# A higher place in the instruction order for carries, the last tile and finished node tiles in a max-pooling layer

## The chip, the cores and the metric

The kernel runs on one core of a Trainium2 chip. A core has several engines that run at the same time, each through its own fixed list of instructions: TensorE (PE in the profile, matrix products; PEld is its weight load), VectorE (DVE, element-wise work and scans), ScalarE (ACT, casts and copies), GpSimd (POOL, here mostly gathers of rows by index) and SyncE (SP, here a queue that starts transfers). Transfers run on 16 DMA engines. An instruction starts when it is its turn on its engine and the semaphores that it waits for have been set. The metric is the device time of one launch in microseconds (us); lower is better.

## The reference

The input is a graph of 6250 nodes with 256 features and 100000 edges, sorted by destination. A normalised copy of the features goes through four graph layers with 512 features between them, then a last product, and the input is added:

```python
def _sage_pool(h, src, dst, n, deg, W_pool, b_pool, W_self, W_neigh, b):
    hp = jax.nn.relu(h @ W_pool + b_pool)
    hmax = jax.ops.segment_max(hp[src], dst, num_segments=n)
    hmax = jnp.where(deg[:, None] > 0, hmax, 0.0)
    return h @ W_self + hmax @ W_neigh + b
...
deg = jax.ops.segment_sum(jnp.ones(edge_dst.shape[0], features.dtype), edge_dst, num_segments=n)
h = _sage_mean(features, edge_src, edge_dst, n, deg, W1_self, W1_neigh, b1)
h = _sage_pool(h, edge_src, edge_dst, n, deg, W2_pool, b2_pool, W2_self, W2_neigh, b2)
h = _sage_gcn(h, edge_src, edge_dst, n, deg, W3_neigh, b3)
h = _sage_mean(h, edge_src, edge_dst, n, deg, W4_self, W4_neigh, b4)
return h @ W_fc + b_fc
```

`_sage_mean` and `_sage_gcn` sum rows over the edges and multiply by weights. Layer 2, the max-pooling layer, takes for each node the maximum over the rows of its in-edges. The change lies in layer 2.

## The kernel before

**Tiles.** The nodes are 49 tiles of 128 rows. Layer 2 reads the row of each edge's source from a table in HBM with gathers of 128 rows (128x512 in float32); there are 782 of them, in six blocks of 52, 100, 220, 180, 130 and 100 gathers. The blocks are taken from the last to the first, so block 5 comes first and block 0 last.

**The loop over gathers.** In a block each of the 128 partitions walks along its own run of edges. A gather (line 1639, on POOL) brings one edge for each partition into `X`, and DVE keeps a running maximum over edges of the same destination (line 1620, function `step`): `run` is the maximum so far, `X` becomes what is stored. A buffer `X` holds two gathers; there are six such buffers. The results go to HBM on SP (line 1624).

**The carry.** A destination's edges can continue from one partition into the next. At a block's end, `carry(b, ...)` turns the last result of the block with PE (`ptcf`, line 1374), scans along the partitions on DVE (`segf`, `cTf`, lines 1387 and 1391), gathers the rows that are to be mended (`fixf`, line 1404, on POOL), turns the scan back on PE (`pcf`, line 1412; 1398 in block 0), takes the maximum (line 1415) and stores the rows (line 1416). In block 0 the rows stay in SBUF.

**Finished node tiles.** When the carry of a block is done, all node tiles whose first edges lie in it can be finished, by `done2(d)`: gathers of the tile's maxima (`tot`, line 1500), a turn (`pt_hTf`, line 1524), products with the weights (`pm_prf`, lines 1531, 1534, 1537), and a split of the result into three bfloat16 parts `hi`, `mid`, `lo` (casts on ACT at 1545, 1554, 1561, with a matmul that subtracts the part between them, 1551 and 1558). The parts are stored to `tab_r`, from which layer 3 reads. `last_done2(d)` does the same for tile 0, which needs block 0's carry: `pc_last` and `pt_last` bring in block 0 (lines 1476 and 1458), `pm_last` is the product (lines 1451, 1484, 1492).

**Early products.** Layer 3 needs, for each destination tile, the sum over source tiles of a matrix of edge counts times the rows that layer 2 has just finished. For 18 destination tiles and source tiles 10 to 41 this is done while layer 2 still gathers: always when four source tiles are finished, a batch of products is put on a list (`pd`, line 571, and 569 for the tile itself), 12 matmuls for each destination and batch. The counts `ae` are loaded on SP (line 1590), the sums are added to `acc3` on DVE (line 1296; the first batch is copied by ACT, line 1299). The finished rows of a tile lie in one of 11 places, `d % 11`, so tiles 2, 1 and 0 write where tiles 13, 12 and 11 of the last batch lay, which the last batch's products must have read.

**What sets the order.** The Python code is a set of generators, of which the loop over gathers takes a piece at a time; this gives each instruction a number, its place in the program. A scheduler then makes each engine's list by simulating readiness: among the instructions that are ready it takes the one with the lowest number. `tc.high_priority(offset=n)` lowers the numbers in its scope by `n`. Before the change no piece of carry, last tile or finished tile is raised by it in this stage, so they and the early products are taken in the order in which the loop emits them:

```python
for g in list(now):
    if next(g, 0) == 0:
        now.remove(g)
```

`now` holds the node tiles under way. Behind the loop, the rest of the generators is run out, and layer 3 begins, whose first loads and gathers (`zt`, line 1745; `ring`, line 488) wait for the last store to `tab_r`.

Of the kernel before, what the change touches and what calls it, by code (L numbers as in the profile page):

```python
# [77 lines left out]
def fast_path(  # L78
# [1012 lines left out]
    with ExitStack() as on:  # L1091
# [35 lines left out]
        def done1(d, acc):  # L1127
# [37 lines left out]
            with behind(ended):  # L1165
                for k in range(KI):
# [11 lines left out]
                        lambda acc, d=d: todo.append(done1(d, acc)), extra=3)  # L1178
# [127 lines left out]
    with tc.tile_pool(name="fl2c", bufs=1) as ck, ExitStack() as late:  # L1306
# [61 lines left out]
        top = late.enter_context(ExitStack())  # L1368
        wpool = top.enter_context(tc.tile_pool(name="fw2", bufs=1))

        def carry(b, last):
            pt = bank(pst, "pt", "ptcf")
            for k in range(KH):
                turn = nc.tensor.transpose(pt[:, k * P : (k + 1) * P],
                                           last[:, k * P : (k + 1) * P], ident)
            if b == 0:
                last_turn.append(turn)
                for f in between:
                    f(KI)
            yield  # L1380
            yield
            yield
            cT = wk.tile([P, KH, P], F32, name="cTf", bufs=1)
            for k in range(KH):
                seg = wk.tile([P, P + 1], F32, name="segf", bufs=2)
                nc.vector.memset(seg[:, 0:1], 0.0)
                nc.vector.tensor_tensor_scan(
                    seg[:, 1:], keepT[:, b, :], pt[:, k * P : (k + 1) * P], 0.0,
                    op0=ALU.mult, op1=ALU.max,
                )  # L1390
                nc.vector.tensor_mul(cT[:, k, :], seg[:, :P], contT[:, b, :])
                yield
            fix = wk.tile([P, FH], F32, name="fixf", bufs=1)
            if b == 0:
                pc = bank(psm, "pm", "pcf")
                for k in range(KH):
                    tc.keep_in_program_order(
                        nc.tensor.transpose(pc[:, k * P : (k + 1) * P], cT[:, k, :], ident))
                for f in between:
                    f(2 * KI)  # L1400
                nc.scalar.copy(fix, pc)
                carried.append(fix)
                return
            nc.gpsimd.indirect_dma_start(
                out=fix, out_offset=None, in_=rows2[0 : run_at[b] + n_of[b] - P, :],
                in_offset=bass.IndirectOffsetOnAxis(ap=fixI[:, b : b + 1], axis=0),
            )
            for _ in range(4):
                yield
            pc = bank(psm, "pm", "pcf")  # L1410
            for k in range(KH):
                nc.tensor.transpose(pc[:, k * P : (k + 1) * P], cT[:, k, :], ident)
            for _ in range(3):
                yield
            nc.vector.tensor_tensor(fix, fix, pc, op=ALU.max)
            nc.sync.dma_start(runs[b][n_of[b] - P :, :], fix)
            for _ in range(4):
                yield
# [212 lines left out]
        for b in reversed(range(NB)):  # L1631
            tb = BLOCKS[b]
            t0 = offs[b] // P
            run = psr.tile([P, FH], F32, name="run")
            for s0 in range(0, tb, G2):
                X = (xmore if at // G2 % 2 else xpool).tile([P, G2, FH], F32, name="X2")
                for k in range(G2):
                    t = t0 + s0 + k
                    nc.gpsimd.indirect_dma_start(  # L1639
                        out=X[:, k, :], out_offset=None, in_=tab_p,  # L1640
                        in_offset=bass.IndirectOffsetOnAxis(ap=srcI[:, t : t + 1], axis=0),
                    )
                    row, st = X[:, k, :], same[:, t : t + 1]
                    if s0 + G2 >= tb:
                        step(row, X[:, 0, :] if k else run, st, row)
                        if k:
                            stored(b, s0 // 2, X)
                    elif k == 0 and s0:
                        step(run, run, st, row)
                    elif k:  # L1650
                        held = run if s0 else X[:, 0, :]
                        if s0 == 0:
                            step(run, held, st, row)
                        step(X[:, 0, :], row, st, held)
                        if s0:
                            step(run, run, st, row)
                        stored(b, s0 // 2, X[:, :1, :])
                    at += 1
                    if at > 8:
                        next(steps, None)  # L1660
                        if todo and next(todo[0], 0) == 0:
                            todo.pop(0)
                    if at >= 130 and at % 12 == 0:
                        next(finding, None)
                    if at == MADE_AT:
                        for _ in steps:
                            pass
                        top.close()
                        early_pool.append(
                            top.enter_context(tc.tile_pool(name="early3", bufs=1)))  # L1670
                    if at <= EARLY_AT:
                        hub.advance(math.ceil(len(first) * max(0, at - 16) / (EARLY_AT - 16)))
                    if copies and not hub.left():
                        copies.pop(0)()
                    early.advance(early.done + math.ceil(
                        early.left() / max(1, min(32, T - 24 - at))))
                    if b == 0 and s0 == 0 and k == 0:
                        for _ in finding:
                            pass
                    if b == 0 and not tiles and not ends and last_tiles and at >= T - 14:  # L1680
                        now += [last_done2(d) for d in last_tiles]
                        last_tiles.clear()
                    if s0 + k > 2 and ends and next(ends[0], 0) == 0:
                        ends.pop(0)
                        tiles += [d for d in reversed(range(NT)) if b_of[d][0] == last_b]
                    if (tiles and not (b and ends) and at >= begun_at + (11 if b else 7)
                            and begun2 < NT * (at - FIRST_AT) / (T - 36 - FIRST_AT)):
                        begun_at = at
                        now.append(done2(tiles.pop(0)))
                        begun2 += 1  # L1690
                    for g in list(now):
                        if next(g, 0) == 0:
                            now.remove(g)
            end = carry(b, X[:, 1, :])
            next(end)
            ends.append(end)
            last_b = b
# [787 lines left out]
```

## Time and profile before

| | |
|---|---|
| time, median of 3 runs | 3219.61 us (3212.12 to 3224.33) |
| the profiled execution | 3232.3 us, span 3230.2 us |
| mean clock of TensorE that the throttle granted | 0.907 |
| busy: PE, DVE, POOL, ACT | 2547.1, 2082.5, 1915.0, 910.9 us |
| first and last gather of layer 2 | 852.9 and 2225.8 us from the span's start |
| last step of the running maximum | 2239.5 us |
| first gather of layer 3 | 2263.9 us |

Rows of the profile name the engine, the line, the operation and the tiles, output first (`pd<-kept_rows,ae`), then the number of instructions (`x30`). In a row of the timeline the first number is the start and the second the length, both in us; in brackets stands how long the engine was idle before and what ended that. In a list of waits the three numbers behind a row are total, times and longest. Ends of matmuls are modelled, so start-to-start distances are the safer measure of their pace. "remote" or "another core or an unknown queue" is a wait whose release the trace doesn't show; on one core it is no other core.

### The profile page before, as it was taken

The numbers are of one execution on the slowest core, as the hardware profiler recorded it, in microseconds if no ns is written. First come the engines' busy times: TensorE is split into PE (matmuls) and PEld (weight loads), VectorE is DVE, ScalarE is ACT, GpSimd is POOL, SyncE is SP. The second block draws the span as 40 slices with busy tenths as digits, with TensorE's granted clock in tenths as the row PEclk, the third lists the DMA queues.
The fourth block names the chain that finished last, engine by engine and source line by source line (L and its number), as shares of the span: only waits on it lengthen the run. The fifth ranks groups of instructions, "written<-read, shape, count | busy, mean of one in ns | idle before, by whom it ended". The sixth has DMA issues, their size and how long they took to land.

```text
span 3230.2 us, 39608 instructions
## 1 busy us (share of the span) xinstructions
PE 2547.1 (79%) x11759; PEld 1330.1 (41%) x11894; DVE 2082.5 (64%) x5526; ACT 910.9 (28%) x2192; POOL 1915.0 (59%) x2238
## 2 busy tenths in 40 slices
PE   4687888898566456587887788798899999888887
PEld 2245555566333222233333333344344444444443
DVE  8677656655567768756776778766356665355555
ACT  5455666653266757511010001011000011000000
POOL 5566666666454655655565556663666665666664
PEclk8799899999898677788998889899999999999998
DMA  8455566666687888878898889886999998767775
GB/s 265 142 169 157 170 176 176 185 186 177 203 284 260 265 266 283 298 261 265 279 297 260 276 269 300 282 273 228 331 325 342 336 348 284 235 200 202 204 205 167
DMA packets 352573, 793.55 MB, mean 246 GB/s; under 512 B 58414, under 2 KB 154134, under 8 KB 352316
## 3 DMA queue, kind: packets, MB, share of 16 engines
q0 software_dynamic: 143840, 502.78, 50.7%
q1 hardware_dynamic: 141208, 205.28, 17.7%
q10 hardware_dynamic: 67300, 82.87, 7.8%
q8 instruction: 96, 1.57, 0.2%
q14 instruction: 129, 1.06, 0.1%
HBM read 592.60 MB, written 198.91 MB: 245 GB/s over the span
## 4 chain that ended last, share of the span: by engine, by line
PE 56%; issue 12%; DVE 9%; another core or an unknown queue 7%; ACT 6%; DMA 5%; POOL 2%; ACTq 0%; SPq 0%; DVEq 0%; POOLq 0%
PE pd L571 16%; PE pg L510 10%; PE pd L563 5%; PE pm_prf L1537 3%; PE pd L564 3%; DVE run L1620 3%; PE pm_hp L1167 2%; PE pb L346 2%; PE pg L505 2%; PE pm_hp L1161 2%; PE pm_w L272 2%; DMA X<-rows,srcIf 2%; PE pm_prf L1531 1%; PE pm_prf L1534 1%
## 5 line engine op out<-in xcount | busy, mean ns | idle before, releaser
L1639 POOL DMA_INDIRECT X<-rows,srcIf x782 | 742.0, 949 | 525.1 <-issue 231.3
L488 POOL DMA_INDIRECT ring<-tab_h,srcT x474 | 454.8, 959 | 274.8 <-issue 97.6
L1620 DVE SCALAR_TENSOR_TENSOR run<-run,samef,X 128x512 f32<-128x512 f32 x758 | 572.2, 755 | 68.2 <-DMA X<-rows,srcIf 43.0
L510 PE MATMUL pg<-ring,hot 128*128 128x256 bf16 (+2 forms) x2348 | 507.4, 323 | 36.0 <-issue 20.8
L571 PE MATMUL pd<-kept_rows,ae 128*128 128x512 bf16 x1523 | 405.8, 403 | 123.5 <-DVE acc L1296 67.2
L541 DVE SCALAR_TENSOR_TENSOR acc<-pg,M,acc 128x256 f32<-128x256 f32 (+2 forms) x681 | 347.3, 535 | 149.9 <-PE pg L510 52.3
L488 POOL DMA_INDIRECT ring<-tab_r,srcE x314 | 309.8, 987 | 172.7 <-issue 70.2
L488 POOL DMA_INDIRECT ring<-tab_s,srcE x314 | 299.9, 955 | 183.0 <-issue 69.7
L571 PEld LDWEIGHTS <-ae 128*128 128x128 fp8e4 x1728 | 176.3, 102 | 395.0 <-issue 247.3
L510 PEld LDWEIGHTS <-hot 128*128 128x128 bf16 x2364 | 235.6, 100 | 244.1 <-issue 109.6
L563 PE MATMUL pd<-zt,ac 128*128 128x512 bf16 x837 | 296.4, 385 | 26.1 <-issue 23.8
L484 DVE TENSOR_SCALAR hot<-iota_bf,keyE 128x128 bf16<-128x128 bf16 x628 | 152.4, 271 | 252.3 <-PE pg L510 76.7
L1620 DVE SCALAR_TENSOR_TENSOR X<-X,samef,run 128x512 f32<-128x512 f32 x379 | 282.3, 745 | 33.3 <-DMA X<-rows,srcIf 16.8
L564 PE MATMUL pd<-zt,ac 128*128 128x256 bf16 x882 | 243.2, 276 | 24.9 <-issue 22.7
L1537 PE MATMUL pm_prf<-unf,hTf 128*128 128x512 f32 x384 | 203.0, 656 | 11.5 <-ACT hTf L1527 6.1
L571 PE MATMUL pd<-Z,A 128*128 128x256 bf16 (+1 forms) x1176 | 195.4, 283 | 16.9 <-issue 14.9
L338 ACT ACTIVATE hs<-ht,onef 128x128 bf16<-128x128 bf16 x396 | 153.7, 393 | 177.8 <-PE pb L346 99.4
L346 PE MATMUL pb<-hm,hs 128*128 128x392 bf16 x461 | 153.6, 350 | 50.0 <-DVE hm L340 21.0
L340 DVE TENSOR_SCALAR hm<-iota_w,mk 128x392 bf16<-128x392 f16 x461 | 151.2, 335 | 47.1 <-PE pb L346 20.9
L1296 DVE TENSOR_TENSOR acc<-acc,pd 128x512 f32<-128x512 f32 x126 | 86.0, 682 | 147.9 <-remote 99.4
L484 DVE TENSOR_SCALAR hot<-iota_bf,keyT 128x128 bf16<-128x128 bf16 x474 | 123.2, 271 | 82.9 <-PE pb L346 32.3
L571 PE MATMUL pd<-kept_rows,ac 128*128 128x512 bf16 x526 | 149.4, 386 | 7.6 <-issue 6.9
(379 smaller groups left out, 3766.1 us busy)
## 6 DMA issues: line engine op xcount, KB each, us to landing
rows<-X SPq DMA_DIRECT2D x385, 256.0 KB
tab_r<-kept_rows ACTq DMA_DIRECT2D x44, 384.0 KB
rows<-hpf SPq DMA_DIRECT2D x49, 256.0 KB
th<-tab_t ACTq DMA_DIRECT2D x49, 256.0 KB
X<-rows,srcIf POOLq DMA_INDIRECT x782
ac<-tab_a ACTq DMA_DIRECT2D x108, 112.0 KB
tab_t<-th SPq DMA_DIRECT2D x37, 256.0 KB
tab_h<-Z SPq DMA_DIRECT2D x16, 579.0 KB
```

The lines of the kernel that those rows point to most:

```text
L338: nc.scalar.activation(hots[0], t, AF.Relu, bias=one, scale=-1.0)
L346: nc.tensor.matmul(hold[0], hots[0], hots[1], start=(k == 0), stop=(k == k_of[w] - 1))
L484: nc.vector.tensor_scalar(hot[j], iota_b, keyT[:, j - jb : j - jb + 1], None, op0=ALU.is_equal)
L488: nc.gpsimd.indirect_dma_start(out=ring[:, j % deep, :], out_offset=None, in_=table, in_offset=bass.IndirectOffsetOnAxis(ap=srcT[:, j - jb ...
L510: mm = nc.tensor.matmul(pg[:, : F + c], hot[j], X[:, part * F : (part + 1) * F + c], start=(k == 0 and part == 2), stop=(k == n - 1 and pa ...
L541: nc.vector.scalar_tensor_tensor(acc[d], half, m, acc[d], op0=ALU.mult, op1=ALU.add)
L563: nc.tensor.matmul(hold[0], a, z[:, : 2 * F], start=(s == ss[0]), stop=False)
L564: nc.tensor.matmul(hold[0][:, :F], a, z[:, 2 * F :], start=False, stop=(s == ss[-1]))
L571: nc.tensor.matmul(hold[0][:, : F + c], a, z[:, part * F : (part + 1) * F + c], start=(s == ss[0] and part == 2 and s != own), stop=(s == ...
L1537: nc.tensor.matmul(pm, hT[:, c, :], un[:, c, :], start=False, stop=(c == KH - 1))
L1620: nc.vector.scalar_tensor_tensor(put, held, st, row, op0=ALU.mult, op1=ALU.max)
L1639: nc.gpsimd.indirect_dma_start(out=X[:, k, :], out_offset=None, in_=tab_p, in_offset=bass.IndirectOffsetOnAxis(ap=srcI[:, t : t + 1], axis=0),
```

## The change

A wrapper `soon` runs each piece of a generator with its numbers lowered, by 2000 where nothing is said, by 600 for finished node tiles. It is put around the carries, around tile 0's generator and around `done2` in the loop. Not wrapped are the early products, and the generators that start only behind the loop.

```diff
+        def soon(pieces, by=2000):
+            while True:
+                with tc.high_priority(offset=by):
+                    if next(pieces, 0) == 0:
+                        return
+                yield
+
         def carry(b, last):
...
                     if b == 0 and not tiles and not ends and last_tiles and at >= T - 14:
-                        now += [last_done2(d) for d in last_tiles]
+                        now += [soon(last_done2(d)) for d in last_tiles]
                         last_tiles.clear()
...
                         begun_at = at
-                        now.append(done2(tiles.pop(0)))
+                        now.append(soon(done2(tiles.pop(0)), 600))
                         begun2 += 1
...
-            end = carry(b, X[:, 1, :])
+            end = soon(carry(b, X[:, 1, :]))
             next(end)
```

Seven lines are added ahead of the rest, so a line above 1371 has a number higher by 7 after the change. Each engine runs the same instructions as before, in another order, and only inside layer 2. Three places show it.

PE at the end of layer 2, before the change. `ptcf` is the last carry's turn (block 0), `pcf` its way back, `pc_last`, `pt_last` and `pm_last` belong to tile 0, `pm_prf` and `pt_hTf` to the node tiles before it:

```order
L1537 MATMUL pm_prf_19869<-unf_10820,hTf_19862 128x512 x4
L1458 MATMUL pt_hTf_19939<-identf_96,tot_19909 128x128 x4
L1374 MATMUL ptcf_19969<-identf_96,X2_19963 128x128 x4
L1451 MATMUL pm_last_19913<-usA_10818,th2_19911 128x512 x2
L1398 MATMUL pcf_19994<-identf_96,cTf_19976 128x128 x3
L1551 LDWEIGHTS minus_b_103
L1551 MATMUL pm_prf_19869<-kept_rows_10802,minus_b_103 128x512
L1398 MATMUL pcf_19994<-identf_96,cTf_19976 128x128
L1451 MATMUL pm_last_19913<-usB_10819,th2_19911 128x512 x2
L1476 MATMUL pc_last_20005<-takes0_17112,fixf_19993 128x128 x4
```

After the change the same place begins so,

```order
L1381 MATMUL ptcf_19969<-identf_96,X2_19963 128x128 x4
L1458 MATMUL pm_last_19913<-usA_10818,th2_19911 128x512 x2
L571 LDWEIGHTS ae_19221
L571 MATMUL pd_19332<-kept_rows_10802,ae_19221 128x512
L1405 MATMUL pcf_19994<-identf_96,cTf_19976 128x128 x4
L1458 MATMUL pm_last_19913<-usB_10819,th2_19911 128x512 x2
```

and, 242 rows of early products further on, ends so:

```order
L571 LDWEIGHTS ae_19512
L571 MATMUL pd_19689<-kept_rows_10802,ae_19512 128x512
L1558 LDWEIGHTS minus_b_103
L1558 MATMUL pm_prf_19869<-kept_rows_10802,minus_b_103 128x512
L1483 MATMUL pc_last_20005<-takes0_17112,fixf_19993 128x128 x4
```

Between the turn and `pc_last` there are now 124 matmuls of early products, 112 of line 571 and 12 of line 569; before there was none.

DVE at the same place. The scans and products of the carry (`segf`, `cTf`) were followed at once by tile 0's maxima (`hTf`):

```order
L1387 TENSOR_SCALAR segf_19989<-keepTf_10825,ptcf_19969 128x128
L1391 TENSOR_TENSOR cTf_19976<-segf_19985,contTf_10826 128x128
L1391 TENSOR_TENSOR cTf_19976<-segf_19989,contTf_10826 128x128
L1479 TENSOR_TENSOR hTf_19914<-hTf_19914,pc_last_20005 128x512
L1482 TENSOR_TENSOR hTf_19914<-hTf_19914,pt_last_20011 128x512
```

After the change ten adds of early products stand between them, of which five rows are shown (the last two and the row behind them follow each other directly):

```order
L1398 TENSOR_TENSOR cTf_19976<-segf_19989,contTf_10826 128x128
L1296 TENSOR_TENSOR acc3_8_10792<-acc3_8_10792,pd_19332 128x512
L1296 TENSOR_TENSOR acc3_9_10793<-acc3_9_10793,pd_19364 128x512
...
L1296 TENSOR_TENSOR acc3_16_10800<-acc3_16_10800,pd_19632 128x512
L1296 TENSOR_TENSOR acc3_17_10801<-acc3_17_10801,pd_19689 128x512
L1486 TENSOR_TENSOR hTf_19914<-hTf_19914,pc_last_20005 128x512
```

Before, the last of all these adds stood 14 steps of the running maximum ahead of the last one; over the stage they stand some 65 steps later than before.

POOL behind the carry of block 4 (`fixf` is the carry's gather, `tot` those of finished tiles). Before, 30 gathers of edges lie between the carry's gather and the first `tot`; the row of `fixf` and the rows around the first `tot` are:

```order
L1404 DMA fixf<-rows_71,fixIf 128x512
L1639 DMA X_14472<-rows_71,srcIf 128x512 x2
L1639 DMA X_14452<-rows_71,srcIf 128x512 x2
...
L1639 DMA X_14647<-rows_71,srcIf 128x512 x2
L1500 DMA tot<-rows_71,rows_of_130 128x512
L1500 DMA tot<-rows_71,rows_of_131 128x512
```

After the change there are six:

```order
L1411 DMA fixf<-rows_71,fixIf 128x512
L1646 DMA X_14452<-rows_71,srcIf 128x512 x2
L1646 DMA X_14472<-rows_71,srcIf 128x512 x2
L1646 DMA X_14489<-rows_71,srcIf 128x512 x2
L1507 DMA tot<-rows_71,rows_of_130 128x512
L1507 DMA tot<-rows_71,rows_of_131 128x512
L1507 DMA tot<-rows_71,rows_of_130 128x512
L1507 DMA tot<-rows_71,rows_of_131 128x512
L1646 DMA X_14504<-rows_71,srcIf 128x512 x2
```

The gathers of finished tiles have moved closer to the carry's gather and stand in a row of four, and two pairs of edge gathers that were exchanged stand in program order.

## The prediction

> **What bounds the kernel now.** The change touches only layer 2's max-pool stage, so I read that stage, 1345 to 2245 us of the span, and the hand-over to layer 3 behind it. First the table by windows (busy time of each engine, granted clock, DMA share), the last three stretches of the stage:
>
> ```profile
> core 0: us, PE busy (x) PEld busy (x) DVE busy (x) ACT busy (x) POOL busy (x), PEclk, DMA share, GB/s
> ...
> 1345.00:1660.00 315.00, 245.81 (x857) 109.59 (x875) 215.82 (x306) 36.18 (x66) 180.20 (x191) 0.89 0.83 273
> 1660.00:2060.00 400.00, 329.06 (x1212) 147.86 (x1235) 298.92 (x439) 34.72 (x60) 235.20 (x249) 0.91 0.86 280
> 2060.00:2245.00 185.00, 152.64 (x489) 69.67 (x494) 125.90 (x198) 23.00 (x41) 106.28 (x113) 0.90 0.83 272
> ```
>
> No engine is full: PE is 78 to 83% busy, DVE 68 to 75%, POOL 57 to 59%, the DMA engines 83 to 86%. The same view by block of gathers, for the gathers of line 1639 alone (blocks 5, 4, 3, 2, 1, 0):
>
> ```profile
> 852.90:1031.90 179.00, 94.87 (x100) 0.85 0.81 267
> 1031.90:1269.50 237.60, 124.28 (x130) 0.68 0.82 269
> 1269.50:1588.40 318.90, 170.39 (x180) 0.83 0.84 277
> 1588.40:1967.60 379.20, 208.41 (x221) 0.92 0.86 279
> 1967.60:2146.00 178.40, 94.48 (x101) 0.89 0.86 279
> 2146.00:2225.80 79.80, 48.57 (x52) 0.91 0.86 286
> ```
>
> Time over gathers is 1.79, 1.83, 1.77, 1.72, 1.77 and 1.53 us for one gather. Blocks 5 and 4 run before the early products begin (about 1345), blocks 3 to 1 beside them, at no slower pace. So the early products do not set the pace of the gathers by themselves. The chain of waits between 1280 and 2264 says that it passes from engine to engine:
>
> ```profile
> by line: PE pd L571 21.3%; another core or an unknown queue 17.4%; issue 13.9%; DVE run L1620 8.4%; PE pm_prf L1537 8.1%; DMA X<-rows,srcIf 5.1%; PE pm_prf L1531 3.6%; PE pm_prf L1534 3.4%; DVE X L1620 3.3%; DMA rows<-X 2.2%; DMA zt<-tab_r
> ```
>
> And the waits in the same window, by engine (total us, times, longest):
>
> ```profile
> DVE acc L1296 <- remote: 99.4, 19, 13.4
> ...
> POOL X L1639 <- DVE run L1620: 80.0, 41, 8.6
> ...
> POOL X L1639 <- DMA rows<-X: 31.4, 29, 7.5
> ...
> PE pd L571 <- DVE acc L1296: 72.7, 17, 10.7
> ...
> PE pm_prf L1551 <- ACT kept_rows L1545: 17.9, 2, 13.7
> ...
> SPq L1590 <- remote: 147.8, 20, 13.8
> ```
>
> DVE stands before the add of an early product (L1296) and the max steps queue behind it; the gathers wait for a buffer that a max step frees; PE waits for DVE to empty a bank; SP waits to load a block of edge counts (L1590) with stores queued behind. It is a loop of waits with slack on every engine. The end of the stage is different, a plain chain (last max step on DVE, then PE, then the first gather of layer 3 on POOL):
>
> ```profile
> 2239.53 0.75 DVE L1620 SCALAR_TENSOR_TENSOR X<-X,samef 128x512 f32<-128x512 f32 x1
> ...
> 2245.79 0.60 PE L1374 MATMUL ptcf<-identf,X 128*128 128x128 f32 x4
> ...
> 2247.95 1.17 PE L1398 MATMUL pcf<-identf,cTf 128*128 128x128 f32 x4
> ...
> 2250.68 1.05 PE L1476 MATMUL pc_last<-takes,fixf 128*128 128x128 f32 x8
> 2251.57 0.60 PE L1458 MATMUL pt_last<-identf,tot 128*128 128x128 f32 x4
> ...
> 2253.37 3.70 PE L1484 MATMUL pm_last<-unf,hTf 128*128 128x512 f32 x8 [0.99 <-DVE hTf L1482]
> 2257.74 0.38 PE L1492 MATMUL pm_last<-kept_rows,minus_b 128*128 128x512 bf16 x1 [0.67 <-ACT kept_rows L1488]
> ...
> 2263.88 0.95 POOL L488 DMA_INDIRECT ring<-tab_r,srcE  x1 [18.86 <-DMA ac<-tab_a]
> ```
>
> From the end of the last max step (2240.3) to layer 3's first gather (2263.9) 23.6 us pass, in which no early product runs. The first 5.5 us are PE's backlog of finished node tiles before the last carry's turn (L1374).
>
> **The change, part by part.** It adds and removes no instruction. Carries and last tile go 2000 places up, finished tiles 600; what loses is the early products, on PE, DVE and SP.
>
> *The tail on PE.* In the new order 124 matmuls of early products (112 of L571, 12 of L569) stand between the last carry's turn and pc_last of tile 0; before there are none. Turn, pc_last and pm_last cannot start before the last max step, and the three last tiles write to rows that the last batch of early products still reads, so this work cannot slip behind. Its price is the spacing of runs of such matmuls, start to next start:
>
> ```profile
> 2030.54 6.64 PE L571 MATMUL pd<-kept_rows,ae 128*128 128x512 bf16 x30
> 2037.02 0.38 PE L1558 MATMUL pm_prf<-kept_rows,minus_b 128*128 128x512 bf16 x1
> ...
> 1704.87 10.64 PE L571 MATMUL pd<-kept_rows,ae 128*128 128x512 bf16 x41
> 1715.36 0.38 PE L1558 MATMUL pm_prf<-kept_rows,minus_b 128*128 128x512 bf16 x1
> ...
> 2261.33 5.64 PE L571 MATMUL pd<-kept_rows,ac 128*128 128x512 bf16 x18
> ```
>
> 6.48 / 30 = 0.216, 10.49 / 41 = 0.256, 5.64 / 18 = 0.313 us. I take 0.216, since the operands in the tail have long been loaded: 124 x 0.216 = 26.8 us. Bounds: 124 x 0.313 = 38.8 us above, and 20 us below, if a quarter of them runs while PE would wait for the scans and casts anyway. Behind the last product come the casts of tiles 2 and 1 into the freed rows; two round trips between PE and ACT at the 0.67 us of the row at 2257.74 add 1.3 us. What goes is the backlog, 5.5 us, because nothing but products is left there. The adds on DVE that now stand behind the last max step, ten of them, keep pace: one is 0.68 us,
>
> ```profile
> 2060.58 0.68 DVE L1296 TENSOR_TENSOR acc<-acc,pd 128x512 f32<-128x512 f32 x1
> ```
>
> and the twelve products that feed it are 12 x 0.216 = 2.6 us; the last add lies beside the casts. Sum of the tail: 26.8 + 1.3 - 5.5 = +22.6 us, bounds 20 + 1.3 - 5.5 = +16 and 38.8 + 1.3 - 5.5 = +35. The work ahead of layer 3's zt loads and gathers is otherwise the same, so all of layer 3 starts that much later after the last max step.
>
> A rule of the Trainium skill speaks for this term: "TensorE: Matmul & The Clock Gate", Part 3, says that matmuls start and end in program order, with no reordering. By it pc_last cannot pass one of the 124; were they free to wait, the tail would gain the 5.5 us. No row here shows a matmul passing another.
>
> *The carries.* Until its turn a block's last result occupies a sixth of the X buffers. Last max step and turn of blocks 3, 2 and 1:
>
> ```profile
> 1601.07 0.75 DVE L1620 SCALAR_TENSOR_TENSOR X<-X,samef 128x512 f32<-128x512 f32 x1
> ...
> 1661.39 0.60 PE L1374 MATMUL ptcf<-identf,X 128*128 128x128 f32 x4
> ...
> 1976.62 0.75 DVE L1620 SCALAR_TENSOR_TENSOR X<-X,samef 128x512 f32<-128x512 f32 x1
> ...
> 2060.95 0.60 PE L1374 MATMUL ptcf<-identf,X 128*128 128x128 f32 x4
> ...
> 2153.10 0.75 DVE L1620 SCALAR_TENSOR_TENSOR X<-X,samef 128x512 f32<-128x512 f32 x1
> ...
> 2199.51 0.60 PE L1374 MATMUL ptcf<-identf,X 128*128 128x128 f32 x4
> ```
>
> That is 60, 84 and 46 us, 190 in all, and the new order shortens it. But block 1's hold lies wholly in block 0, whose pace, 1.53 us, is the best of all; block 2's hold fills 84 of the 178 us of block 1, at 1.77 us, no slower than block 4 with no long hold (1.83). So I take 0. Bounds: a sixth of 190 = 32 us gained; nothing lost. Earlier carries let node tiles begin earlier, which moves work on PE but does not end anything, as the products behind them end last now: 0.
>
> *Finished tiles ahead of products.* On POOL the first gather of tot follows the carry's gather after 6, 6, 14, 6 and 20 other gathers, before it is 12, 30, 58, 56 and 42. POOL issues in order, so a tot gather whose carry is not yet stored stops the X gathers behind it. Five carries; at worst each waits for ten gathers' worth, 10 x 1.77 = 18 us, 88 us in all; at best 0, where turn, scan and max come as much earlier as their order says. They are all pieces of the same higher place, so I take 0 to 10 and put 5 into the sum. On PE, tiles now run with fewer products between a cast and the matmul on it: by the order 22 of 48 tiles have under 1.5 us of other matmuls between L1537 and L1551, before it is 9, and between L1551 and L1558 16 against 6. That is 23 more tight round trips, at 0.67 us 15 us of PE time, at 1.2 us (the 17.9 us above over the 15 tight ones of before) 28 us. PE is idle 17 to 22% of the stage anyway, so of these I count 0, with 28 as the bound. On DVE the adds of products come some 65 max steps later, and SP loads the counts some 20 stores later, which moves the waits of 99.4 and 147.8 us above: gain and loss are both open. I take 0; the bounds are half of 99.4 gained, 50, and PE's 72.7 us wait for DVE half as long again, 36 lost.
>
> *What goes out from ahead of the last turn.* 26.8 + 5.5 = 32 us of PE work. Where PE is in the chain for some 36% (pd and the three pm_prf) of the stage this could bring the last max step forward by 0.36 x 32 = 12 us, and by 32 at the most. I take 5, no more, since the gathers' pace was the same without products.
>
> **Sum.** +22.6 (tail) + 5 (POOL) - 5 (less PE work before) = +23 us. The profiled execution takes 3232.3 us with a span of 3230.2, the median of the runs is 3219.6: 3255 us by the profile's own time, 3243 by the median.
>
> **The rivals.**
> 1. *It evens out, about 3216.* If PE sets the pace after all, moving products to the tail moves time and adds none: the stage before gains the 26.8 us that the tail receives, and the backlog saves some more, -4. For it: PE and its release make up the larger part of the chain. DVE's waits on "remote" have no recorded releaser, and "Perfetto Trace Analysis", section "Tensor Engine Instruction", says that the end of a matmul is estimated by the profiler, while the release comes only when PSUM acknowledges its bytes. So PE may be fuller than the 82% shown. Against it: blocks without products are no faster.
> 2. *Faster, about 3193.* DVE's adds of products no longer stop the max steps. If half of the 99.4 us goes, the stage gains 50 and the tail gives back 23: -27. It decides the sign from 23 of the 99.4 us on, the measurable gain from 39. For it: the adds stand 65 steps later. Against it: their products stand later on PE too.
> 3. *Slower still, about 3271.* The tight round trips cost PE 28 us that come on top of the tail, if PE's idle time does not lie where they fall; or POOL stops before the tots.
> 4. *No change*, that instructions do not move, is excluded by the order.
>
> **How the numbers follow.** Forecast (+16 to +40 us, 3236 to 3260): 0.44. Rival 1: 0.24. Rival 2: 0.18. Rival 3: 0.14. Half a per cent, 16 us, is about what a measurement of this kernel can tell from no change. Slower by more: 0.44 + 0.14 = 0.58; same 0.24; faster 0.18. The range leaves out half of rival 2 and the upper third of rival 3: 3195 to 3282.
>
> **What would show it.** In the changed profile: over 20 us of L571 between the last ptcf and pc_last, and 42 to 58 us from the last max step to the first ring gather; the last max step within 15 us of 2240. Holds of blocks 3 to 1 under 30 us with the same 1.7 to 1.8 us for one gather would show that they cost nothing. If the gathers of blocks 3 to 1 come under 1.65 us, a loop of waits was opened and I am wrong on the fast side; if POOL waits over 10 us before tots, or PE's waits at L1551 (now L1558) sum to over 40, on the slow side.

## The result: slower by one and a half per cent

The changed kernel takes 3261.13 us (median of 4 runs, 3255.99 to 3277.54), the kernel before 3216.07 us (4 runs, 3212.12 to 3224.33). The ratio is 1.0148, 95% interval 1.0121 to 1.0175: 45 us slower. The forecast was slower by 23 us, 3243, with a range of 3195 to 3282. The profiled execution of the changed kernel takes 3277.5 us with a span of 3275.6, 45.4 us over that of the kernel before, so the two profiles show the same difference as the medians.

The end of layer 2 in the changed kernel's timeline (last max step on DVE, then PE, then the first gather of layer 3 on POOL; lines above 1371 are higher by 7):

```profile
2262.59 0.74 DVE L1627 SCALAR_TENSOR_TENSOR X<-X,samef 128x512 f32<-128x512 f32 x1
...
2263.48 0.63 PE L1381 MATMUL ptcf<-identf,X 128*128 128x128 f32 x4 [0.89 <-DVE X L1627]
...
2266.00 0.71 PE L1405 MATMUL pcf<-identf,cTf 128*128 128x128 f32 x4
...
2295.03 1.05 PE L1483 MATMUL pc_last<-takes,fixf 128*128 128x128 f32 x8
...
2298.37 3.70 PE L1491 MATMUL pm_last<-unf,hTf 128*128 128x512 f32 x8 [0.56 <-DVE hTf L1489]
...
2308.51 0.95 POOL L488 DMA_INDIRECT ring<-tab_r,srcE  x1 [40.49 <-issue]
```

From the end of the last max step (2263.3) to the first gather of layer 3 it is 45.2 us, before it was 23.6: +21.6. The last max step itself comes 23.1 us later than before (2262.6 against 2239.5). Together they are 44.7 of the 45.4 us; layers 3 and 4 add the rest. So about half of the loss is where the forecast put all of it, and half is in the gather phase, for which the forecast had summed to nothing.

The gather phase by stretches of the same view as before, and by block of gathers (line 1646):

```profile
1345.00:1660.00 315.00, 218.57 (x693) 96.93 (x706) 195.16 (x292) 54.28 (x104) 175.08 (x184) 0.85 0.79 262
1660.00:2060.00 400.00, 331.42 (x1209) 148.29 (x1230) 295.56 (x434) 34.88 (x62) 235.91 (x249) 0.92 0.85 275
```

```profile
851.30:1021.10 169.80, 95.06 (x100) 0.85 0.85 279
1021.10:1256.10 235.00, 123.60 (x131) 0.69 0.84 278
1256.10:1584.80 328.70, 170.86 (x181) 0.77 0.80 267
1584.80:1980.80 396.00, 208.65 (x220) 0.90 0.83 268
1980.80:2164.70 183.90, 95.58 (x101) 0.91 0.83 272
2164.70:2245.50 80.80, 48.51 (x51) 0.91 0.87 293
```

Blocks 5 and 4 are not slower; in this pair of traces they are 9 and 3 us shorter. Blocks 3, 2 and 1 take 328.7, 396.0 and 183.9 us where they took 318.9, 379.2 and 178.4: +32 us in the three blocks that run beside early products. In the second pair of traces, taken later (see the experiments), the same three blocks take 30 us more. Between 1345 and 1660 PE does 218.6 us of work where it did 245.8, 27 us less.

The holds of the X buffer are gone in blocks 3, 2 and 1, under 1 us each from the end of the last max step to the turn. In block 2 the two rows now start 1.3 us apart (84 before):

```profile
1985.48 0.75 DVE L1627 SCALAR_TENSOR_TENSOR X<-X,samef 128x512 f32<-128x512 f32 x1
...
1986.81 0.60 PE L1381 MATMUL ptcf<-identf,X 128*128 128x128 f32 x4
```

### The profile page after: what moved, and what is told of

The parts are those of the page before. It is cut to its first block, busy times and chain, and to the rows that moved or that the text cites. A ratio compares the mean times of both kernels' runs of the same rounds, so it can differ in the third digit from the quotient of the medians.

```text
span 3275.6 us, 39589 instructions
## 1 busy us (share of the span) xinstructions
PE 2547.2 (78%) x11759; PEld 1334.9 (41%) x11894; DVE 2088.2 (64%) x5526; ACT 910.8 (28%) x2192; POOL 1918.4 (59%) x2238
## 3 DMA queue, kind: packets, MB, share of 16 engines
q0 software_dynamic: 143840, 502.78, 49.8%
## 4 chain that ended last, share of the span: by engine, by line
PE 53%; issue 13%; DVE 10%; another core or an unknown queue 9%; ACT 5%; DMA 5%; POOL 2%; ACTq 1%; DVEq 0%; POOLq 0%; SPq 0%
PE pd L571 14%; PE pg L510 10%; PE pd L563 5%; DVE run L1627 4%; PE pd L564 3%; PE pm_w L272 3%; PE pm_hp L1167 2%; PE pb L346 2%; PE pm_hp L1161 2%; PE pg L505 2%; PE pm_prf L1544 2%; DVE X L1627 2%; POOL X L1646 2%; PE pm_prf L1538 1%
## 5 line engine op out<-in xcount | busy, mean ns | idle before, releaser
L1544 PE MATMUL pm_prf<-unf,hTf 128*128 128x512 f32 x384 | 188.5, 613 | 1.5 <-ACT hTf L1534 1.2
L390 PE MATMUL pb<-hm,hs 128*128 128x196 bf16 x320 | 64.0, 303 | 120.1 <-ACT A L395 47.1
```

The source lines that it names most:

```text
L1544: nc.tensor.matmul(pm, hT[:, c, :], un[:, c, :], start=False, stop=(c == KH - 1))
```

## The experiments

They ran in three series of four, which the record lists under three different chips. The kernel before takes 3183.73, 3182.87 and 3185.47 us in them, and each ratio is against the runs of the kernel before in the same series. Each run has one trace, so a stretch of a trace is weaker evidence than a ratio. The edits are against the changed kernel unless it is said otherwise.

**Is it the products that stand behind the last turn?** The wrapper is taken off the last tile:

```diff
-                        now += [soon(last_done2(d)) for d in last_tiles]
+                        now += [last_done2(d) for d in last_tiles]
```

> The wrapper is taken off the last tile alone; carries and finished tiles keep it. The orders of POOL and SP are those of the changed kernel in every row, those of PE, DVE and ACT up to the last 10 us of the stage; no early product stands behind the last carry's turn any more, they stand ahead of it. Theory (124 products wait in the tail while PE had time for them before): the stretch from the last max step to layer 3's first gather goes back from 45 us to about 24 and the time from 3261 to about 3239. Rival (PE is behind with its work when the last max step comes, so the same products then delay the turn instead): the stretch stays at 42 to 50 us and the time at 3255 to 3265.

Measured: 3224.40 us, ratio 1.0142 (1.0091 to 1.0194). The end of layer 2 in its timeline:

```profile
2217.26 0.74 DVE L1627 SCALAR_TENSOR_TENSOR X<-X,samef 128x512 f32<-128x512 f32 x1
...
2242.87 2.11 PE L571 MATMUL pd<-kept_rows,ae 128*128 128x512 bf16 x9
...
2246.09 0.66 PE L1381 MATMUL ptcf<-identf,X 128*128 128x128 f32 x4 [0.28 <-ACT hTf L1475]
...
2251.12 1.05 PE L1483 MATMUL pc_last<-takes,fixf 128*128 128x128 f32 x8
...
2264.16 0.94 POOL L488 DMA_INDIRECT ring<-tab_r,srcE  x1 [41.44 <-DMA ac<-tab_a]
```

The products now stand ahead of the turn, and the turn waits for them: it comes 28.1 us after the end of the last max step, and from there to the first gather it is 46.2 us, where the changed kernel has 45.2. The rival was right. The place of the products behind the turn costs nothing by itself; in both orders PE still has them to do when the last max step is done.

**Which of the three wrappers?** Carries alone first:

```diff
-                        now.append(soon(done2(tiles.pop(0)), 600))
+                        now.append(done2(tiles.pop(0)))
...
-                        now += [soon(last_done2(d)) for d in last_tiles]
+                        now += [last_done2(d) for d in last_tiles]
```

> Only the carries are wrapped; finished tiles and the last tile are as before the change. Theory (the loss in the gather phase comes from finished tiles that run ahead of early products): no loss, the last max step near 2240 us, the time within 3208 to 3222. Rival 1 (earlier carries themselves disturb the gathers): about 3235. Rival 2 (the held X buffer costs time): up to 30 us faster than before, 3186 to 3205.

Measured: 3195.56 us, ratio 1.0021 (0.9997 to 1.0046): no gain, and no loss that can be told from none. It doesn't tell what a freed buffer is worth, because the buffer is hardly freed. In its trace the turns of blocks 3, 2 and 1 still come 59, 23 and 37 us after the end of the last max step, against 64, 79 and 41 us in the kernel before, run again below. Its profiled execution was the longest of its runs, 10 us over their median, so the last max step at 2224.5 us (1382.4 after the first gather) says little.

Finished tiles alone:

```diff
-            end = soon(carry(b, X[:, 1, :]))
+            end = carry(b, X[:, 1, :])
...
-                        now += [soon(last_done2(d)) for d in last_tiles]
+                        now += [last_done2(d) for d in last_tiles]
```

> Only finished node tiles are wrapped (600 places). There are no early products behind the last turn. Theory: the gather phase loses what it lost in the changed kernel, some 23 us, and the tail nothing: 3230 to 3245, last max step near 2262 us. Rival (the loss needs the earlier carries): 3210 to 3222.

Measured: 3232.45 us, ratio 1.0145 (1.0110 to 1.0180). The finished tiles make the whole loss alone. But it isn't where I expected it: the last max step comes early, at 2215.9 us, and the first gather of layer 3 66 us later, with PE working through tiles and products that were left:

```profile
2215.92 0.75 DVE L1627 SCALAR_TENSOR_TENSOR X<-X,samef 128x512 f32<-128x512 f32 x1 [0.22 <-DMA X<-rows,srcIf]
...
2264.54 0.60 PE L1381 MATMUL ptcf<-identf,X 128*128 128x128 f32 x4
...
2282.27 0.95 POOL L488 DMA_INDIRECT ring<-tab_r,srcE  x1 [31.78 <-issue]
```

So the split between gather phase and end is not fixed; what is lost in one kernel before the last max step is lost in another behind it.

**Products raised with the tiles.** All three wrappers stay:

```diff
-                    early.advance(early.done + math.ceil(
-                        early.left() / max(1, min(32, T - 24 - at))))
+                    with tc.high_priority(offset=600):
+                        early.advance(early.done + math.ceil(
+                            early.left() / max(1, min(32, T - 24 - at))))
```

> All three wrappers stay, and the early products that the loop emits get 600 places as well, so that finished tiles and products stand to each other as before while the carries stay early. No product stands behind the last turn. Theory (products that come late on PE hold up DVE's adds and with them the max steps): the time goes back to that of before, 3205 to 3225, and DVE's waits before the adds to 150 us or less in 1280 to 2264. Rival (POOL's earlier gathers of tot or the early carries cost the time): 3235 to 3245, with only the tail's 22 us gone.

Measured: 3201.86 us, ratio 1.0063 (1.0033 to 1.0094), between the two expectations: about half of the loss is gone when products and tiles keep their old rank to each other. DVE's waits before the adds are 124 us from the first gather to the last max step, inside the 150 that the theory named; the changed kernel, run again, has 146, so this says little.

**Early tiles or late tiles?** The profile of the changed kernel shows PE idle for long between 1200 and 1400 us, while the blocks of edge counts (L390, tile pb) and the first tiles compete. That gave a theory A, that the loss is made there once and carried to the end, against theory B, that it is made all through the stage by PE's waits for casts.

```diff
-                        now.append(soon(done2(tiles.pop(0)), 600))
+                        now.append(soon(done2(tiles.pop(0)), 600) if at > EARLY_AT else done2(tiles.pop(0)))
```

> As the changed kernel, but a finished tile is wrapped only if it begins after gather 250; the tiles of block 5 and the first of block 4 are left as before the change. Theory A (the loss is made ahead of 1400 us: raised tiles push back the blocks of edge counts of line 390 and the first early products start 40 to 80 us late, and PE never makes up for it): the time is close to before, ratio 0.999 to 1.006, with the first add or copy of an early product (L1296, L1299) at most 15 us later than before. Theory B (tiles that run ahead of products all through the stage cost it, by PE that waits for casts): ratio 1.009 to 1.015.

Measured: 3217.31 us, ratio 1.0106 (1.0056 to 1.0156). By the ratio this is theory B. But the test did not do what theory A needed: the first copy of an early product comes 71 us later after the first gather than in the kernel before, not at most 15. Now the complement:

```diff
-                        now.append(soon(done2(tiles.pop(0)), 600))
+                        now.append(soon(done2(tiles.pop(0)), 600) if at <= EARLY_AT else done2(tiles.pop(0)))
```

> The complement: a finished tile is wrapped only if it begins up to gather 250, all later ones are as before the change; carries and the last tile are wrapped. Theory A: the loss is here, ratio 1.008 to 1.015, PE's busy time in 1200 to 1400 us about 40 us under that of the kernel with raised carries alone (127 us). Theory B: ratio 1.000 to 1.005.

Measured: 3192.58 us, ratio 1.0025 (0.9998 to 1.0053). The early tiles, raised without the late ones, cost nothing that can be told from none. PE does do 37 us less between 1200 and 1400 us (89.7 us, with carries alone 127.0), as theory A expected, but the time doesn't follow. The late tiles cost more, some seven tenths of the loss by the middle of a wide interval.

One half of theory A falls with that, the blame on the early tiles. The other half stays: a late start of the early products goes with the late tiles. The copies of the first sums (line 1299), in the kernel before run again, with late tiles raised, and with early tiles raised (first and last start behind the durations in ns; first gathers at 849.8, 848.8 and 842.3 us):

```profile
L1299 ACT COPY acc<-pd x18: 585/585/592, 1366.2 to 1466.0; 128x512 f32<-128x512 f32 x18
```

```profile
L1299 ACT COPY acc<-pd x18: 586/586/603, 1436.5 to 1522.2; 128x512 f32<-128x512 f32 x18
```

```profile
L1299 ACT COPY acc<-pd x18: 585/585/605, 1363.4 to 1464.7; 128x512 f32<-128x512 f32 x18
```

No run raises only the tiles that begin after the products are under way, so the start and what follows it are not told apart.

**The kernel before, for its trace:**

> The kernel before itself, for a trace beside these: ratio 0.997 to 1.003; 22 to 26 us from the last max step to layer 3's first gather.

Measured: 3186.71 us, ratio 1.0005 (0.9968 to 1.0041); 23.5 us from the last max step to the first gather.

**The opposite order.** Carries and last tile raised, products raised by 600, tiles not:

```diff
-                        now.append(soon(done2(tiles.pop(0)), 600))
+                        now.append(done2(tiles.pop(0)))
...
-                    early.advance(early.done + math.ceil(
-                        early.left() / max(1, min(32, T - 24 - at))))
+                    with tc.high_priority(offset=600):
+                        early.advance(early.done + math.ceil(
+                            early.left() / max(1, min(32, T - 24 - at))))
```

> Carries and the last tile are wrapped as in the change, finished tiles are not, and the early products get 600 places instead. By the theory that PE's unfinished products at the last max step set the end, products that come earlier leave less of them: the last add some 50 us ahead of the last max step, and a ratio of 0.992 to 1.000. Rival (tiles that come later give the next products later, so nothing is won): 1.000 to 1.006.

Measured: 3212.08 us, ratio 1.0083 (1.0054 to 1.0113). Both expectations missed: products ahead of tiles cost too, though these products are not late. Here the last add does come early (2153.8, some 75 us ahead of the last max step), but PE stands at the first subtracting matmul for casts, 99.0 us in this window (1250 to 2280), where the kernel before has 6.9. Rows of the view by line, this kernel first, the last part being idle time and its releasers:

```profile
L1558 PE MATMUL pm_prf<-kept_rows,minus_b 128*128 128x512 bf16 x38 | 16.5, 434 | 99.0 <-ACT kept_rows L1552 67.2 <-issue 31.6
```

```profile
L1551 PE MATMUL pm_prf<-kept_rows,minus_b 128*128 128x512 bf16 x39 | 17.1, 438 | 6.9 <-issue 4.5 <-ACT kept_rows L1545 2.4
```

**Is it the wait for casts?** In the second trace of the changed kernel (the last run below) that row stands at 66.7 us, which speaks for theory B. To test it, the tile is raised only up to its first cast, so that products stand between cast and matmul again:

```diff
         def soon(pieces, by=2000):
+            n = 0
             while True:
-                with tc.high_priority(offset=by):
+                n += 1
+                with tc.high_priority(offset=by) if by > 600 or n <= 16 else nullcontext():
                     if next(pieces, 0) == 0:
```

> As the changed kernel, but a finished tile is raised only up to the cast of hi; the two subtracting matmuls, mid, lo and the store keep their place, so that early products stand between a cast and the matmul on it again (in the order 10 and 6 tight places instead of 19 and 19), though products still come later than before. No product stands behind the last turn. Theory B (PE's waits at pm_prf for casts make the loss): PE's idle time at pm_prf back from 110 to 50 to 70 us, ratio 1.000 to 1.006. Theory C (it is the lateness of the products, whatever PE waits for): ratio 1.010 to 1.015.

Measured: 3225.68 us, ratio 1.0140 (1.0100 to 1.0181). PE's wait at the first subtracting matmul for its cast, from the first gather of layer 2 to the end of the stage, in the list of waits of this kernel, of the changed kernel and of the kernel before, the two others run again:

```profile
PE pm_prf L1560 <- ACT kept_rows L1554: 16.6, 3, 13.1
```

```profile
PE pm_prf L1558 <- ACT kept_rows L1552: 72.5, 10, 13.3
```

```profile
PE pm_prf L1551 <- ACT kept_rows L1545: 3.2, 2, 2.4
```

Most of the wait is gone. All of PE's idle time at `pm_prf`, summed over the rows of the list from the first gather to the last max step, is 51.5 us here, 121.1 in the changed kernel and 49.8 in the kernel before: it went back as theory B asked, and the time has not moved. So these waits are not what makes the loss in the changed kernel. Some of the idle time has come up elsewhere: before the turns of finished tiles (`pt_hTf`) it is 58.4 us here, 14.2 in the changed kernel and 35.3 in the kernel before. What stays as it was in the changed kernel is that the first part of each tile stands ahead of products.

The same, with the tiles up to gather 250 not raised:

```diff
-                        now.append(soon(done2(tiles.pop(0)), 600))
+                        now.append(soon(done2(tiles.pop(0)), 600) if at > EARLY_AT else done2(tiles.pop(0)))
```

> The same, and the tiles that begin up to gather 250 not raised at all, which leaves the blocks of edge counts (pb) ahead of them as before the change. Theory B: PE's idle time at pm_prf 50 to 70 us and at pb 75 to 100, ratio 0.998 to 1.004. Theory C: 1.006 to 1.012, as with late tiles raised whole (1.0106).

Measured: 3217.50 us, ratio 1.0100 (1.0056 to 1.0145), as with the late tiles raised whole (1.0106). Theory C, lateness of the products, is the one that expected both.

**Close casts alone, in the kernel before:**

```diff
         def apart_by(n):
-            for _ in range(n):
+            for _ in range(0):
                 yield
```

> The kernel before, with no spacing of pieces around the subtracting matmuls (the three waits of 3, 2 and 3 pieces are set to none); nothing is raised and the products stand where they stood. In the order the second matmul follows the first closely in 32 tiles instead of 7. Theory B: PE's idle time at pm_prf rises by 15 to 40 us and the ratio is 1.003 to 1.012. Theory C: 0.998 to 1.003.

Measured: 3202.42 us, ratio 1.0054 (1.0027 to 1.0080). The middle lies inside theory B's range and outside theory C's; PE's idle time at `pm_prf` is 92.6 us, 43 more than in the kernel before run again. The edit empties all four waits of a finished tile (3, 2, 3 and 2 pieces; the expectation counts three), so a tile is also finished ten pieces earlier, and the cost is not shown to be the closeness alone. It is about a third of the changed kernel's loss, and by the two runs before not what makes it there.

**The changed kernel again, for its trace:**

> The changed kernel again, for a trace on the chip of these runs: ratio 1.011 to 1.018; PE idle some 40 us more between the first gather of layer 2 and pc_last than in the kernel before, most of it at pm_prf and pb; 42 to 48 us from the last max step to layer 3's first gather.

Measured: 3227.65 us, ratio 1.0133 (1.0090 to 1.0177). PE is idle 59 us more than in the kernel before from the first gather to the last max step (411.0 against 351.9), more than expected; 71 us more at `pm_prf`, 31 more at `pb`, and less elsewhere.

**What lateness looks like.** The matmuls of line 571 in two windows of the trace (count behind the second number), first the kernel before, then the late tiles raised up to their cast, then the changed kernel, all three from these series; their first gathers lie within 3 us:

```profile
1340.00:1800.00 460.00, 244.82 (x943) 96.90 (x944) 0.91 0.87 285
1800.00:2100.00 300.00, 156.06 (x624) 62.41 (x623) 0.91 0.87 282
```

```profile
1340.00:1800.00 460.00, 216.39 (x864) 88.30 (x864) 0.89 0.84 274
1800.00:2100.00 300.00, 162.94 (x646) 65.92 (x646) 0.90 0.85 271
```

```profile
1340.00:1800.00 460.00, 214.16 (x837) 85.12 (x837) 0.89 0.84 273
1800.00:2100.00 300.00, 145.41 (x558) 56.83 (x558) 0.90 0.85 276
```

| kernel | products by 1800 us | last max step to first gather, us | first copy of a product, us after layer 2's first gather | ratio |
|---|---|---|---|---|
| before, again | 943 | 23.5 | 516 | 1.0005 |
| carries alone | 937 | 22 | 518 | 1.0021 |
| early tiles raised | 916 | 39 | 521 | 1.0025 |
| before, casts close | 951 | 37 | 528 | 1.0054 |
| products raised too | 888 | 42 | 552 | 1.0063 |
| products ahead of tiles | 934 | 29 | 515 | 1.0083 |
| late tiles, up to the cast | 864 | 33 | 543 | 1.0100 |
| late tiles | 839 | 29 | 588 | 1.0106 |
| the change, again | 837 | 45 | 586 | 1.0133 |
| tiles up to the cast | 857 | 39 | 552 | 1.0140 |
| last tile not raised | 837 | 46 | 585 | 1.0142 |
| tiles alone | 837 | 66 | 590 | 1.0145 |

All kernels with a ratio of 1.010 or more have done at most 864 products by then, all others at least 888; among the others the count gives no order. The last max step to the first gather, the forecast's term, orders them much worse. The first copy shows that the lateness begins with the products: 69 to 74 us later than in the kernel before where late tiles are raised whole and products are not, 27 and 36 where they are raised up to the cast. But a late start does not set the time by itself, as 552 stands at both 1.0063 and 1.0140.

The first pair of traces has 856 of these matmuls in the window before the change and 739 after it (882 and 762 weight loads; some matmul records are missing there), and first copies at 531 and 594 us. The direction is the same, but the kernel before lies under 864 there, so the counts can be compared only among the twelve kernels of the table. Nor do they say which way the effect runs: a batch of products can begin only when its four tiles are finished, and these need the gathers.

And where PE's work is when the last max step is done: the kernel before and the changed kernel, both run again, from last max step to first gather:

```profile
2202.30:2225.80 23.50, 20.56 (x69) 9.66 (x68) 5.86 (x27) 5.07 (x9) 0.94 (x1) 0.93 0.37 115
```

```profile
2236.30:2281.70 45.40, 42.55 (x179) 19.22 (x180) 12.67 (x36) 5.66 (x10) 0.94 (x1) 0.97 0.19 60
```

PE is busy 20.6 of 23.5 us and 42.6 of 45.4: the stretch is little longer than PE's work in it, which is 22 us more in the changed kernel. As much and more was left undone earlier: between the last max steps of blocks 4 and 3 the kernel before has PE busy 228.8 of 308.0 us, the changed kernel 201.9 of 324.1. The granted clock there (behind POOL's figures) is 0.85 and 0.78; the kernel with early tiles raised has 0.79 in the same stretch and hardly any loss.

```profile
1260.30:1568.30 308.00, 228.76 (x776) 101.83 (x775) 217.21 (x367) 77.82 (x155) 186.79 (x197) 0.85 0.88 290
```

```profile
1253.40:1577.50 324.10, 201.90 (x662) 93.67 (x662) 213.82 (x373) 106.51 (x224) 188.17 (x200) 0.78 0.83 273
```

## Why the prediction was right, and where it was not

The direction was right and the size about half: +23 us forecast, +45 measured. The cause was wrong in part, and the direction owes something to luck: the forecast rested on products that stand behind the last turn, and the same loss comes without them there (ratio 1.0142).

- **The tail, +22.6 us (bounds +16 to +35): measured +21.6, the path as forecast, the reason wrong.** All but one of the 124 products run from 2268.27 to 2294.82 us with no gap, 26.6 us where 26.8 was taken for all of them, and the turn comes at once when the last max step is done, as forecast. But the step said that these products cost because they stand behind the turn. With the last tile's wrapper off they stand ahead of it and the stretch is as long. The rule of the Trainium skill that the prediction named ("TensorE: Matmul & The Clock Gate", Part 3, matmuls keep program order) agrees with the trace: pc_last starts at 2295.03, behind the last run of products, which starts at 2292.87; it tells that pc_last waits, not that the wait costs. The right reading is the one that rival 1 had at its root: what counts is how much work PE has left, not where in its list it stands. My mistake was to treat work put in front of the last turn as free, because PE showed 17 to 22% idle time; with the products ahead of the turn that idle time did not take them in. That the number agrees is luck in part, as the stretch runs from 29 to 66 us among kernels with a ratio of 1.010 or more.
- **The gather phase, +5 - 5 = 0: measured +23 us in the first profile.** Here the sum was mis-sized. The forecast noted that DVE's adds come 65 max steps later and called gain and loss both open (50 gained to 36 lost), and took 0. The runs show a loss: with only the finished tiles after gather 250 raised, beside carries and last tile, the ratio is 1.0106. No gain of 5 us for less PE work ahead of the last turn can be seen. The argument behind the small terms was that blocks beside early products (1.72 to 1.77 us for one gather) ran no slower than blocks without (1.79 and 1.83). It told how well the old order fitted, not what another order would do: 1.80 to 1.84 us after the change.
- **The carries, 0: not contradicted, but not tested.** In the changed kernel the holds are gone and the blocks got slower, not faster. With carries alone (1.0021) the holds of blocks 3 and 1 stayed nearly as long as before, and every kernel whose three holds are all short also raises the late tiles. So the bound of 32 us to be gained is open.
- **Close round trips between PE and ACT, counted as 0 with 28 us as the bound: the wait was mis-sized, its part in the time is about 0.** In the first two traces PE's waits for the first cast rose from 20.0 to 60.3 us, and its idle time at all of `pm_prf` from 56.3 to 110.0 us, 54 more, above the bound. Taking them away again changed nothing that can be measured (1.0140). That the kernel before with its casts close is 0.5% slower shows that the 0 is no rule.
- **POOL, +5 us: open.** Its waits before tots, from first gather to last max step, rose from 46 to 58 us in the first pair of traces and from 49 to 67 in the second, more than the 0 to 10 us allowed; no run isolates what they cost.
- **Rival 1** (it evens out) was wrong on the time, its premise on the tail was right. **Rival 2** (DVE's adds no longer stop the max steps) is refuted by sign. **Rival 3** was nearest on the time (3271 against 3261); of its two reasons the run with tiles up to the cast takes away the round trips, and POOL's waits before tots are untested. **Rival 4** was excluded.
- **The signs.** The products behind the last turn and the stretch of 45.2 us came as named. The last max step did not stay within 15 us of 2240 (2262.6). The holds came under 30 us, but with 1.83, 1.80 and 1.84 us for one gather in blocks 3, 2 and 1. Both signs of the slow side came: a wait of 15.7 us on POOL before a tot, and 60.3 us of PE's waits at line 1558.

Two things stay open. That late products slow the gathers is shown only as a correlation, and why they would is not known. DVE's idle time before the adds, from first gather to last max step, is 120 us in the kernel before and 146 in the changed one, both run again, but it is 91 us with tiles alone (1.0145) and 164 us with carries alone (1.0021), so it does not go with the loss; no run takes these waits away alone. And the kernel with early tiles raised has a stretch of 39 us at the end and hardly any loss; its gather phase is shorter (1348 us from first gather to last max step, 1353 before), and what gives it that is not known. None of the kernels tried beats the kernel before.

## What to carry to other kernels

When two streams of work share an in-order engine in a stage that is a loop of waits, a higher place for one of them can be paid by the other, even where every engine shows idle time; here both orders lost, tiles ahead of products and products ahead of tiles. Compare how far each stream has come at fixed times, not only what stands at the end. Before work behind the last dependency is priced as a loss, ask whether it would have been done by then if it stood ahead; an order with it ahead answers that in one run. And a wait that a profile shows to have tripled need not be the cause: taking it away moved the idle time, not the end.

## What was not expected of the hardware

The same kernel, the one before the change, took 3216 us in the first series (median of 4 runs) and 3183 to 3187 us in the later ones, 1% less, so only ratios within one series are compared here. The three later series, listed under three chips, agree within 0.1%. The chip of the first series is not on record, so what makes the 1% is open. Single stretches of traces differ by more: the first 100 gathers took 179.0 us in the first trace of the kernel before and 163.7 us in its second, with one and the same order.
